# Rows of h_prime by a block transpose and a round trip through memory, fused masks in all batches, and the next batch's scores moved to the middle of a batch

## Chip, cores and metric

The kernel runs on one core of a Trainium2 chip. The time is the device time of one launch in microseconds (us); lower is better. The engines are PE (matmuls), DVE (vector), ACT (activations), POOL (GpSimd) and SP (here only a queue that issues DMAs).

## What is computed

Two graph layers over 16 batches of 1024 nodes with 128 features. `adj` is a symmetric 0/1 matrix per batch. Cut to what matters:

```
# layer 0, per batch
h = x @ Ww.T + Wb
e = (h @ A) @ h.T;  e = e + e.T
scores = where(adj > 0, e, 0)
attention = softmax(scores, axis=1) * adj
h_prime = relu(attention @ h)
ic, fc, oc = sigmoid(h_prime @ w_u + x @ w_x)        # three gates, one number per node each
x1 = layernorm(x + oc * tanh(ic * h_prime + fc * x))
# layer 1, per batch, 4 heads
h = x1 @ conv_w[hd] + conv_b[hd]
scores = h @ attn_w[hd] @ h.T
out += relu(tanh(adj * scores) @ h)
x2 = layernorm(x1 + relu(relu(out / 4) + x1))
```

Everything is float32.

## The kernel before

**Tiling.** The 1024 nodes of a batch are 8 blocks of 128 (NB = 8)[...]. A batch's adjacency is 8 tiles of 128x1024 (`adjp`, 16 buffers, so two batches). Only the pool `ps_sc` with four PSUM banks takes the results of the matmuls that are read at once; it is shared by scores, projections and small products. Two accumulators of two banks each (`acc0`, `acc1`) hold the products of layer 0 and layer 1.

**Order.** The order of instructions on each engine is the order in which the program is written; nothing is reordered afterwards. Waits between engines follow from the data and from the reuse of buffers.

**The main loop (lines 619 to 640).** For each batch b there are 32 steps, one for each head and row block. `layer1_step` multiplies one block of scores of layer 1 (PE, L510), weighs it by the adjacency (DVE, L511), takes the tanh (ACT, L512) and queues its product (PE, L516), which is issued two steps later (DELAY = 2). At the end of a head `add_head` (L528) adds the accumulator into the sum. Between the steps stand pieces of layer 0 of the following batch. They are functions with short names, and a table says which run after which step: BETWEEN (L609) for the batch b+1, AHEAD (L615) for the batch b+2, TURN (L616) for the step that turns x1, and ENDING (L617) for the four pieces of the last batch's end (turn of the sum, residual, statistics, normalisation and output).

**Pieces of layer 0** (function `layer0`; j is a row block):

- `L` loads xT and all eight adjacency tiles on SP's queue, `X` loads x.
- `Q0 Q1` project qT (PE, ACT). `H0 H1 H2` project h's rows (PE L272, DVE L273); three columns of the product are the gates' part from x.
- `Sj` makes a block row of scores from its diagonal on (PE L288, ACT L291). They are symmetric, so `Tj` (`turn_score`) brings the rest of block row j in transposed: a DVE transpose of 32x32 blocks (L313), a write to memory (L317) and four reads that set the blocks in place (L320), all on SP. Batch 0 uses PE for it.
- `Aj` (`mask`) masks the scores and takes their maximum. With an edge mask in hand (batch 0, made by `find_edges` on POOL, L328) this is one fused DVE operation (L338) with a read of its accumulator and a negation (L342); otherwise it is two DVE operations (L345, L346). Then ACT takes the exponential (L348).
- `Bj` (`weigh`) multiplies by the adjacency (DVE L353), scales h (L355, ACT L357) and issues the product for block j-1 (PE L365). `R` issues the last one and takes the relu into `hpT`, which has features on the partitions.
- `P`, `p` (`rows_hp`, L377): eight matmuls of `hpT` with `ident_g` (L384), an identity with the three gate columns beside it. They give h_prime with nodes on the partitions and h_prime's part of the gates in the same result; ACT copies them out (L385).
- `G` (`gates`): the sum of the gate parts, the sigmoids (ACT L392, DVE L393, L394) and, on POOL, fc * x (L398).
- `I0`, `O0`, `V0`, `N0`: the inner and outer steps (DVE L408, ACT L412, DVE L419) and the layernorm (statistics L184 to L188, a power on POOL L189, L192).

`turn_x1` and `layer1_end` use the helper `turn` (L221): a DVE transpose (L225), a write to memory (L227), four reads (L230), one directly after the other on SP's queue. SP takes its DMAs in order, and one that waits holds those behind it. Where buffers are few (`R`, `u`, `x`, `hp` one each, `turn` two), a piece waits for the last use of the tile.

Of the kernel before, what the change touches and what calls it, by code (L numbers as in the profile page):

```python
# [11 lines left out]
F32 = mybir.dt.float32  # L12
BF16 = mybir.dt.bfloat16
AF = mybir.ActivationFunctionType
# [4 lines left out]
P = 128  # L19
# [4 lines left out]
def two_layer_adjacency_kernel(  # L24
# [44 lines left out]
    a_in = consts.tile([P, P], F32, name="a_in")  # L69
    nc.sync.dma_start(a_in, A)  # L70
    ww_in = consts.tile([P, P], F32, name="ww_in")
# [19 lines left out]

    def load_late_weights():
        nc.sync.dma_start(cw_in[0:1], conv_b.rearrange("(o h) d -> o h d", o=1))
        nc.sync.dma_start(cw_in[1:P], conv_w[:, 0 : D - 1, :].rearrange("h f d -> f h d"))
        nc.sync.dma_start(cw_last, conv_w[:, D - 1 : D, :].rearrange("h f d -> f h d"))
        nc.sync.dma_start(aw, attn_w.rearrange("h i j -> i h j"))

# [6 lines left out]
    but_first = consts.tile([1, P], F32, name="but_first")  # L104
# [10 lines left out]
    a_sym = consts.tile([P, P], F32, name="a_sym")  # L115
    s_ww = consts.tile([P, P], F32, name="s_ww")
# [3 lines left out]
    b_wide = consts.tile([P, P], F32, name="b_wide")  # L120
# [98 lines left out]
    Q = 32  # L219

    def turn(dst, src, name):  # L221


        t = sb.tile([P, N], F32, tag="turn", name=f"turn_{name}", bufs=2)
        nc.vector.transpose(t.rearrange("p (k d) -> p k d", d=P), src)  # L225
        d = dram.tile([P, N], F32, tag="turn", name=f"dram_{name}")
        nc.sync.dma_start(d, t)  # L227
        dv = d.rearrange("(a i) (k c j) -> c i k a j", i=Q, c=P // Q, j=Q)
        for c in range(P // Q):
            nc.sync.dma_start(  # L230
                dst[ts(c, Q)].rearrange("i (k a j) -> i k a j", a=P // Q, j=Q), dv[c]
            )

    adj_t, x_t, x1_t = {}, {}, {}


    def layer0(b):
# [7 lines left out]
        def load():  # L245
            t["xT"] = sb.tile([P, N], F32, tag="xT", name=f"xT_{b}")
            nc.sync.dma_start(t["xT"], xT[b])
            adj_t[b] = []
            for j in range(NB):
                a = adjp.tile([P, N], F32, tag="adj", name=f"adj_{b}_{j}")  # L250
                nc.sync.dma_start(a, adjT[b, ts(j, P), :])
                adj_t[b].append(a)
# [44 lines left out]
        def turn_score(j):  # L297


            R, L, w = t["R"], NB - 1 - j, (NB - 1 - j) * P  # L300
            if b == 0:
                for l0 in range(0, L, 4):
                    ls = range(j + 1 + l0, min(j + 5 + l0, NB))
                    ps = small(f"turn0_{j}_{l0}")
                    for i, l in enumerate(ls):
                        nc.tensor.transpose(ps[:, ts(i, P)], R[:, l, j, :], ident)
                    nc.scalar.copy(
                        R[:, j, ls[0] : ls[-1] + 1, :],
                        ps[:, : len(ls) * P].rearrange("p (l d) -> p l d", d=P),
                    )  # L310
                return
            sq = sb.tile([P, N], F32, tag="turn", name=f"turn0_{b}_{j}", bufs=2)
            nc.vector.transpose(  # L313
                sq[:, :w].rearrange("p (l d) -> p l d", d=P), R[:, j + 1 :, j, :]
            )
            d = dram.tile([P, w], F32, tag=f"turn0_{j}", name=f"dram0_{b}_{j}")
            nc.sync.dma_start(d, sq[:, :w])  # L317
            dv = d.rearrange("(a i) (l c j) -> c i l a j", i=Q, c=P // Q, j=Q)
            for c in range(P // Q):
                nc.sync.dma_start(  # L320
                    R[ts(c, Q), j, j + 1 :, :].rearrange("i l (a j) -> i l a j", j=Q),
                    dv[c],
                )

        def find_edges(j):

            m = sb.tile([P, N], BF16, tag="h1", name=f"edge_{b}_{j}", bufs=NB + 1)
            nc.gpsimd.tensor_scalar(m, adj_t[b][j], 0.0, None, ALU.is_gt)  # L328
            t["edge", j] = m.rearrange("p (k d) -> p k d", d=P)

        def mask(j):
            s = t["R"][:, :, j, :]
            nmax = sb.tile([P, 1], F32, tag="nmax", name=f"nmax_{b}_{j}", bufs=4)
            if ("edge", j) in t:
                top = -3e38
                for q, ks in enumerate((ts(0, BH), ts(1, BH)) if j == 0 else [slice(NB)]):
                    highest = sb.tile([P, 1], F32, tag="highest", name=f"highest_{b}_{j}_{q}", bufs=4)
                    nc.vector.tensor_tensor_reduce(  # L338
                        s[:, ks], s[:, ks], t["edge", j][:, ks], 1.0, top, ALU.mult, ALU.max, highest
                    )  # L340
                    top = highest
                nc.vector.tensor_scalar_mul(nmax, highest, -1.0)  # L342
            else:
                adj = adj_t[b][j].rearrange("p (k d) -> p k d", d=P)
                nc.vector.scalar_tensor_tensor(s, adj, 0.0, s, op0=ALU.is_gt, op1=ALU.mult)  # L345
                nc.vector.tensor_reduce(nmax, s, AX.XY, ALU.max, negate=True)  # L346
            t["z", j] = sb.tile([P, 1], F32, tag="z", name=f"z_{b}_{j}", bufs=4)
            nc.scalar.activation(s, s, AF.Exp, bias=nmax, accum_out=t["z", j])  # L348

        def weigh(j):  # L350

            s = t["R"][:, :, j, :]
            nc.vector.tensor_mul(s, s, adj_t[b][j].rearrange("p (k d) -> p k d", d=P))  # L353
            rz = sb.tile([P, 1], F32, tag="rz", name=f"rz_{b}_{j}", bufs=4)
            nc.vector.reciprocal(rz, t["z", j])  # L355
            t["hz", j] = sb.tile([P, D], F32, tag="hz", name=f"hz_{b}_{j}", bufs=4)
            nc.scalar.mul(t["hz", j], t["h"][:, j, :D], rz)  # L357
            if j:
                back(j - 1)
# [27 lines left out]
        def gates():  # L387

            gate = t["gate"]
            gflat = gate.rearrange("p k g -> p (k g)")  # L390
            nc.vector.tensor_add(gate, t["hp"][:, :, D : D + 3], gate)
            nc.scalar.activation(gflat, gflat, AF.Exp, scale=-1.0)  # L392
            nc.vector.tensor_scalar_add(gflat, gflat, 1.0)  # L393
            nc.vector.reciprocal(gflat, gflat)  # L394
            t["u"] = sb.tile([P, NB, D], F32, tag="u", name=f"u0_{b}", bufs=1)
            t["x1"] = sb.tile([P, NB, D + 1], F32, tag="x1", name=f"x1_{b}")
            for ks in PARTS:
                nc.gpsimd.tensor_mul(  # L398
                    t["u"][:, ks], t["x"][:, ks],
                    gate[:, ks, 1:2].to_broadcast([P, ks.stop - ks.start, D]),  # L400
                )
            nc.gpsimd.memset(t["x1"][:, :, 0:1], 1.0)

# [21 lines left out]
        def finish(p):  # L425
# [7 lines left out]
            "L": load, "X": load_x, "R": relu,  # L433
            "P": lambda: rows_hp(GROUPS[:-1]), "p": lambda: rows_hp(GROUPS[-1:]),
            "G": gates,
        }
        for i, ks in enumerate(GROUPS):
            pieces[f"H{i}"] = partial(project_h, [ks])
# [7 lines left out]
        for j in range(NB):  # L446
            for name, piece in (("S", score), ("A", mask), ("B", weigh)):
                pieces[f"{name}{j}"] = partial(piece, j)
            if b == 0:
                pieces[f"E{j}"] = partial(find_edges, j)  # L450
# [10 lines left out]
    x1T_t, h1_t, u_t = {}, {}, {}  # L461

    def turn_x1(b):
        if b:
            x1T_t[b] = sb.tile([P, N], F32, tag="x1T", name=f"x1T_{b}")
            turn(x1T_t[b], x1_t[b][:, :, 0:D], f"x1_{b}")
            return
# [25 lines left out]
    def layer1_step(b, hd, m):  # L493
        x1T, h1, uT = x1T_t[b], h1_t[b, m], u_t[b, hd]
        adj = adj_t[b][m]
# [50 lines left out]
    def layer1_end(b):  # L546
        x1 = x1_t[b][:, :, 1 : D + 1]
        y = sb.tile([P, NB, D], F32, tag="u", name=f"y_{b}", bufs=1)
        turn(y.rearrange("p k d -> p (k d)"), sum_t[b].rearrange("p (k d) -> p k d", d=P), f"sum_{b}")
# [8 lines left out]
    def last_end(b, k0, k1):  # L558
# [19 lines left out]
    run(first, "L X")  # L578
    load_late_weights()
    run(second, "L")  # L580
# [8 lines left out]
    run(first, "P p G")  # L589
# [14 lines left out]
    run(second, "T0 T1 T2")  # L604
    rows(0, range(NB))

    BETWEEN = [  # L609
        "H0 H1 H2", "S0", "T0 S1", "T1 S2", "T2 A0", "S3 B0", "T3 A1", "S4 B1",  # L610
        "T4 A2", "S5 B2", "T5 A3", "S6 B3", "T6 A4", "S7 B4", "A5", "B5",
        "A6", "B6", "A7", "B7", "X R", "P", "p G", "I0",
        "O0", "V0", "N0", "", "", "", "", "",
    ]
    AHEAD = {28: "L", 31: "Q0 Q1"}  # L615
    TURN = 27  # L616
    ENDING = (DELAY, DELAY + 3, DELAY + 5, DELAY + 7)  # L617
    end, nxt = None, second
    for b in range(B):
        after = layer0(b + 2) if b + 2 < B else {}  # L620
        for step in range(H * NB):
            hd, m = divmod(step, NB)
            layer1_step(b, hd, m)
            if b and step == 0:
                rows(b, range(NB // 2, NB))
            if end is not None and step in ENDING:
                next(end, None)
            run(nxt, BETWEEN[step])
# [64 lines left out]
```

## Time and profile before

Three runs took 2447.58, 2448.38 and 2449.35 us, a median of 2448.38. The profiled run took 2446.58, and its span is 2444.8 us at a granted PE clock of 0.999.

| group (line) | count | us busy | mean ns of one |
|---|---|---|---|
| PE scores of layer 1 (L510) | 2048 | 962.0 | 592 |
| PE product of layer 1 (L516) | 2016 | 947.3 | 592 |
| PE product of layer 0 (L365) | 512 | 241.1 | 593 |
| PE rows of h_prime (L384) | 256 | 33.8 | 275 |
| DVE scores by adjacency (L511) | 1008 | 671.5 | 685 |
| DVE mask (L345) | 120 | 143.3 | 1195 |
| DVE maximum (L346) | 120 | 146.4 | 1220 |
| DVE fused mask, batch 0, 1024 wide (L338) | 7 | 8.5 | 1210 |
| DVE weights by adjacency (L353) | 128 | 158.7 | 1240 |
| POOL edges, batch 0 (L328) | 8 | 23.4 | 2950 |
| POOL fc * x, 1024 wide (L398) | 15 | 28.5 | 1900 |
| ACT copy of h_prime's rows, 393 wide (L385) | 32 | 15.6 | 488 |

A float32 matmul appears as two records. The time of one record is its latency; records that follow each other overlap, so that the mean of one is longer than the time it adds, and what it adds is the distance between two starts. In a list of waits the columns are the waiting instruction, what it waited for, the sum in us, how often, and the longest.

| DMA | queue | count | KB each | us to landing |
|---|---|---|---|---|
| adjacency tile | SP | 128 | 512 | 7.7 |
| xT | SP | 16 | 512 | 4.5 |
| x1's write, reads | SP | 15, 60 | 512, 128 | 2.6, 3.1 |
| output | POOL | 15 | 512 | 3.5 |

### The profile page before, as it was taken

The numbers are of one execution on the slowest core, as the hardware profiler recorded it, in microseconds if no ns is written. First come the engines' busy times: TensorE is split into PE (matmuls) and PEld (weight loads), VectorE is DVE, ScalarE is ACT, GpSimd is POOL, SyncE is SP. The second block draws the span as 40 slices with busy tenths as digits, with TensorE's granted clock in tenths as the row PEclk, the third lists the DMA queues.
The fourth block names the chain that finished last, engine by engine and source line by source line (L and its number), as shares of the span: only waits on it lengthen the run. The fifth ranks groups of instructions, "written<-read, shape, count | busy, mean of one in ns | idle before, by whom it ended". The sixth has DMA issues, their size and how long they took to land.

```text
span 2444.8 us, 19911 instructions
## 1 busy us (share of the span) xinstructions
PE 2427.2 (99%) x6175; PEld 1121.6 (46%) x6175; DVE 1585.3 (65%) x3026; ACT 1083.9 (44%) x1522; POOL 136.5 (6%) x102
## 2 busy tenths in 40 slices
PE   8999999999999999999999999999999999999998
PEld 4444444444444444444444444444444444444444
DVE  6665847657586565866658666585765857658454
ACT  6444444344444444434444444444444444444432
POOL 4000000000000000000000000000000000000000
PEclk9999999999999999999999999999999999999999
DMA  4204124051230512304133140332404223042000
GB/s 174 60 10 145 45 95 95 1 151 39 95 95 9 148 34 101 89 21 142 27 108 81 52 124 15 119 70 72 106 12 128 62 95 84 11 135 55 17 26 9
DMA packets 409057, 180.77 MB, mean 74 GB/s; under 512 B 352630, under 2 KB 377078, under 8 KB 408951
## 3 DMA queue, kind: packets, MB, share of 16 engines
q1 hardware_dynamic: 405927, 171.63, 25.2%
q0 software_dynamic: 2160, 7.87, 0.8%
q8 instruction: 49, 0.80, 0.1%
q14 instruction: 57, 0.47, 0.1%
q10 hardware_dynamic: 864, 0.00, 0.0%
HBM read 127.80 MB, written 51.64 MB: 73 GB/s over the span
## 4 chain that ended last, share of the span: by engine, by line
PE 94%; DVE 2%; DMA 2%; SPq 1%; issue 0%; POOL 0%; ACT 0%; POOLq 0%; DVEq 0%
PE sc L510 34%; PE acc L516 34%; PE acc L365 9%; PE sc L288 5%; PE pT_u L201 4%; PE pR L481 4%; PE pT_q L201 1%; PE pt L384 1%; PE pR_h L272 1%; DMA xT<-in_xT_dram 1%; SPq L230 1%; DMA dram_x<-turn_x 0%; DVE st L184 0%; DVE x L192 0%; POOL rs L189 0%
## 5 line engine op out<-in xcount | busy, mean ns | idle before, releaser
L511 DVE TENSOR_TENSOR s<-sc,adj 128x512 f32<-128x512 f32 x1008 | 671.5, 685 | 623.0 <-PE sc L510 611.0
L510 PE MATMUL sc<-uT,x1T 128*128 128x512 f32 x2048 | 962.0, 592 | 0.0
L516 PE MATMUL acc<-s,h 128*128 128x512 f32 x2016 | 947.3, 592 | 0.0
L512 ACT ACTIVATE s<-s 128x1024 f32<-128x1024 f32 x504 | 533.0, 1057 | 806.9 <-DVE s L511 800.5
L516 PEld LDWEIGHTS acc<-s,h 128*128 128x128 f32 x2016 | 381.7, 190 | 483.5 <-issue 474.4
L510 PEld LDWEIGHTS sc<-uT,x1T 128*128 128x128 f32 x2048 | 385.7, 190 | 468.8 <-issue 421.7
L365 PE MATMUL acc<-R,hz 128*128 128x512 f32 x512 | 241.1, 593 | 1.5 <-ACT hz L357 1.4
L348 ACT ACTIVATE R<-R,nmax 128x1024 f32<-128x1024 f32 x128 | 147.0, 1149 | 201.9 <-DVE nmax L346 182.2
L353 DVE TENSOR_TENSOR R<-R,adj 128x1024 f32<-128x1024 f32 x128 | 158.7, 1240 | 5.7 <-issue 0.3
L346 DVE TENSOR_REDUCE nmax<-R 128x1 f32<-128x1024 f32 x120 | 146.4, 1220 | 4.1
L288 PE MATMUL sc<-xT,qT 128*128 128x512 f32 (+3 forms) x384 | 146.5, 491 | 0.5 <-ACT R L291 0.5
L365 PEld LDWEIGHTS acc<-R,hz 128*128 128x128 f32 x512 | 95.6, 190 | 108.0 <-issue 85.1
L345 DVE SCALAR_TENSOR_TENSOR R<-adj,R 128x1024 f32<-128x1024 f32 x120 | 143.3, 1195 | 0.0
L189 POOL TENSOR_TENSOR rs<-rs,mhalf 128x8 f32<-128x8 f32 (+2 forms) x35 | 65.8, 1881 | 1207.0 <-DVE rs L188 948.3
L291 ACT ACTIVATE R<-sc,h 128x512 f32<-128x512 f32 (+1 forms) x192 | 109.4, 579 | 39.2 <-PE sc L288 37.7
L201 PE MATMUL pT_u<-x1T,ms 128*128 128x512 f32 x256 | 120.4, 592 | 0.0
L481 PE MATMUL pR<-cw,x1T 128*128 128x512 f32 x256 | 114.9, 592 | 0.0
L357 ACT ACTIVATE hz<-h,rz 128x128 f32<-128x128 f32 x128 | 51.3, 400 | 128.7 <-DVE rz L355 128.4
L288 PEld LDWEIGHTS sc<-xT,qT 128*128 128x128 f32 x384 | 70.1, 192 | 70.4 <-issue 58.0
L484 ACT COPY h<-pR 128x512 f32<-128x512 f32 x128 | 75.0, 586 | 41.7 <-PE pR L481 41.7
L398 POOL TENSOR_TENSOR u<-x,gate 128x1024 f32<-128x1024 f32 (+1 forms) x17 | 30.6, 1799 | 969.4 <-DVE gate L394 969.4
L534 DVE SCALAR_TENSOR_TENSOR sum<-acc,sum 128x512 f32<-128x512 f32 x95 | 61.2, 686 | 33.8 <-PE acc L516 32.9
(109 smaller groups left out, 1035.2 us busy)
## 6 DMA issues: line engine op xcount, KB each, us to landing
adj<-in_adjT_dram SPq DMA_DIRECT2D x128, 512.0 KB, 7.7
xT<-in_xT_dram SPq DMA_DIRECT2D x16, 512.0 KB, 4.5
x<-in_x_dram SPq DMA_DIRECT2D x16, 512.0 KB, 4.2
dram_x<-turn_x SPq DMA_DIRECT2D x15, 512.0 KB, 2.6
x1T<-dram_x SPq DMA_DIRECT2D x60, 128.0 KB, 3.1
dram_sum<-turn_sum SPq DMA_DIRECT2D x15, 512.0 KB, 2.6
y<-dram_sum SPq DMA_DIRECT2D x60, 128.0 KB, 3.1
out_dram<-y POOLq DMA_DIRECT2D x15, 512.0 KB, 3.5
```

The source lines that it names most:

```text
L201: nc.tensor.matmul(ps, w, src[:, ts(q, 512)], start=True, stop=True)
L288: nc.tensor.matmul(ps[:, : at - lo], t["qT"][:, ts(j, P)], t["xT"][:, lo:at], start=True, stop=True)
L345: nc.vector.scalar_tensor_tensor(s, adj, 0.0, s, op0=ALU.is_gt, op1=ALU.mult)
L346: nc.vector.tensor_reduce(nmax, s, AX.XY, ALU.max, negate=True)
L348: nc.scalar.activation(s, s, AF.Exp, bias=nmax, accum_out=t["z", j])
L353: nc.vector.tensor_mul(s, s, adj_t[b][j].rearrange("p (k d) -> p k d", d=P))
L365: nc.tensor.matmul(t["acc"][:, ts(q, 512)], t["hz", j], t["R"][:, ts(q, BH), j, :], start=(j == 0), stop=(j == NB - 1),)
L481: nc.tensor.matmul(ps, x1T_t[b][:, ts(k, P)], cw.rearrange("p h d -> p (h d)"), start=True, stop=True)
L510: nc.tensor.matmul(ps, x1T[:, ts(m, P)], uT[:, ts(q, 512)], start=True, stop=True)
L511: nc.vector.tensor_mul(s[:, ts(q, 512)], ps, adj[:, ts(q, 512)])
L512: nc.scalar.activation(s, s, AF.Tanh)
L516: nc.tensor.matmul(acc[:, ts(q, 512)], h1[:, ts(hd, D)], s[:, ts(q, 512)], start=(m == 0), stop=(m == NB - 1),)
```

## The change

1. **h_prime's rows.** In batches 1 to 15 `hpT` is turned as x1 is: DVE transpose, write, four reads (`turn_hp`, piece P). h_prime's part of the gates then comes from three weighted sums over the features: POOL multiplies by a gate's weights (`weigh_hp`), which are loaded once as rows on all partitions (`wu_b`), and DVE sums (`sum_hp`). The gates are finished in pieces Y, F, i and o. Batch 0 keeps the matmuls.
2. **Masks.** All batches use the fused operation; from batch 1 on the mask is uint8 with two buffers and is made per block (`E0` to `E7`) on POOL.
3. **Hops.** `hop` issues the write to memory and keeps the reads, which `land` issues a step later.
4. **Loads.** xT (W) and each adjacency tile (L0 to L7) are pieces of their own, and from batch 2 on the adjacency comes by POOL's queue.
5. **Plan.** The scores S and turns T of batch b+2 run in steps 15 to 22 of batch b (before: steps 1 to 13 of batch b+1); masks and weights run from step 29 on into steps 0 to 10. The first loop has a plan of its own (FIRST). ENDING is 2, 6, 11, 13 instead of 2, 5, 7, 9.
6. **Buffers.** Some weight tiles of the preparation move into shared buffers.

```diff
+    wu_b = consts.tile([P, 3, D], F32, name="wu_b")
...
+        for g, w in enumerate((wi_u, wf_u, wo_u)):
+            nc.sync.dma_start(wu_b[:, g, :], w.partition_broadcast(P))
...
+    def hop(dst, t, name):
+        d = dram.tile(list(t.shape), F32, tag=f"hop_{t.shape[1]}", name=f"dram_{name}")
+        nc.sync.dma_start(d, t)
+        dv = d.rearrange("(a i) (k c j) -> c i k a j", i=Q, c=P // Q, j=Q)
+        def read():
+            for c in range(P // Q):
+                nc.sync.dma_start(
+                    dst[ts(c, Q)].rearrange("i k (a j) -> i k a j", a=P // Q), dv[c]
+                )
+        hops.append(read)
+    def land():
+        while hops:
+            hops.popleft()()
...
+        def load_adj(j):
+            a = adj_t[b, j] = adjp.tile([P, N], F32, tag="adj", name=f"adj_{b}_{j}")
+            (nc.sync if b < 2 else nc.gpsimd).dma_start(a, adjT[b, ts(j, P), :])
...
         def find_edges(j):
-            m = sb.tile([P, N], BF16, tag="h1", name=f"edge_{b}_{j}", bufs=NB + 1)
-            nc.gpsimd.tensor_scalar(m, adj_t[b][j], 0.0, None, ALU.is_gt)
+            if b == 0:
+                m = sb.tile([P, N], BF16, tag="h1", name=f"edge_{b}_{j}", bufs=NB + 1)
+            else:
+                m = sb.tile([P, N], U8, tag="edge", name=f"edge_{b}_{j}")
+            nc.gpsimd.tensor_scalar(m, adj_t[b, j], 0.0, None, ALU.is_gt)
...
-                nc.vector.scalar_tensor_tensor(s, adj, 0.0, s, op0=ALU.is_gt, op1=ALU.mult)
-                nc.vector.tensor_reduce(nmax, s, AX.XY, ALU.max, negate=True)
+                nc.vector.tensor_tensor_reduce(
+                    s[:, ks], s[:, ks], t["edge", j][:, ks], 1.0, nmax, ALU.mult, ALU.max, top
+                )
...
+        def turn_hp():
+            t["hp"] = sb.tile([P, NB, D], F32, tag="hp", name=f"hp_{b}", bufs=1)
+            hpT = t["hpT"].rearrange("p (k d) -> p k d", d=P)
+            turn(t["hp"], hpT, f"hp_{b}")
+        def weigh_hp(g):
+            if b not in x1T_t:
+                x1T_t[b] = sb.tile([P, N], F32, tag="x1T", name=f"x1T_{b}")
+            t["hw"] = x1T_t[b].rearrange("p (k d) -> p k d", d=P)
+            nc.gpsimd.tensor_mul(
+                t["hw"], t["hp"], wu_b[:, g : g + 1, :].to_broadcast([P, NB, D])
+            )
+        def sum_hp(g):
+            hw = sb.tile([P, NB, 1], F32, tag="hw", name=f"hws_{b}_{g}")
+            nc.vector.tensor_reduce(hw, t["hw"], AX.X, ALU.add)
+            gate = t["gate"][:, :, g : g + 1]
+            nc.vector.tensor_add(gate, hw, gate)
...
+        def gate_f():
+            sum_hp(1)
+            sigmoid(t["gate"][:, :, 1:2])
+            forget()
+            weigh_hp(0)
+        def gate_i():
+            sum_hp(0)
+            weigh_hp(2)
+        def gates_io():
+            sum_hp(2)
+            sigmoid(t["gate"][:, :, 0:3:2])
...
-    run(second, "T0 T1 T2")
+    run(second, "T0 T1")
+    land()
+    run(second, "T2 E0")
     rows(0, range(NB))
+    land()
...
-    BETWEEN = [
-        "H0 H1 H2", "S0", "T0 S1", "T1 S2", "T2 A0", "S3 B0", "T3 A1", "S4 B1",
-        "T4 A2", "S5 B2", "T5 A3", "S6 B3", "T6 A4", "S7 B4", "A5", "B5",
-        "A6", "B6", "A7", "B7", "X R", "P", "p G", "I0",
-        "O0", "V0", "N0", "", "", "", "", "",
-    ]
-    AHEAD = {28: "L", 31: "Q0 Q1"}
-    TURN = 27
-    ENDING = (DELAY, DELAY + 3, DELAY + 5, DELAY + 7)
+    BETWEEN = {
+        0: "L7 E5 B1 A3", 1: "B2", 2: "E6 A4", 3: "E7 B3 A5", 4: "A6", 5: "B4", 7: "B5 A7",
+        8: "B6", 10: "B7", 11: "X R", 12: "P", 14: "Y", 16: "F", 18: "i", 20: "o", 21: "I0",
+        22: "O0", 23: "V0", 24: "N0",
+    }
+    AHEAD = {
+        9: "W", 12: "Q0 Q1", 14: "H0 H1 H2", 15: "S0", 16: "T0 S1", 17: "T1 S2", 18: "T2 S3",
+        19: "T3 S4", 20: "T4 S5", 21: "T5 S6", 22: "T6 S7", 25: "L0", 26: "L1", 27: "L2 E0",
+        28: "L3 E1", 29: "L4 A0 E2", 30: "L5 A1 E3", 31: "L6 B0 A2 E4",
+    }
+    FIRST = {
+        0: "E1 A0 T3 S4", 1: "E2 B0 A1 T4 S5", 2: "E3 A2 T5 S6", 3: "E4 B1 A3 T6 S7",
+        4: "E5 B2 A4", 5: "E6 B3 A5", 6: "E7 B4 A6", 7: "B5 A7",
+    }
+    TURN = 25
+    ENDING = (DELAY, 6, 11, 13)
...
         for step in range(H * NB):
             hd, m = divmod(step, NB)
             layer1_step(b, hd, m)
+            land()
```

## The prediction

> **What bounds the kernel now.** I read the page first: busy time by engine, then the chain that ended last.
>
> ```profile
> span 2444.8 us, 19911 instructions
> PE 2427.2 (99%) x6175; PEld 1121.6 (46%) x6175; DVE 1585.3 (65%) x3026; ACT 1083.9 (44%) x1522; POOL 136.5 (6%) x102
> PE 94%; DVE 2%; DMA 2%; SPq 1%; issue 0%; POOL 0%; ACT 0%; POOLq 0%; DVEq 0%
> ```
>
> PE is busy for all but 17.6 us of 2444.8, and 94% of the last chain is PE. A busy PE need not be at its peak, so I next looked at the timeline of PE around the rows of h_prime, at about 1066 us.
>
> ```profile
> 1064.32 1.88 PE L516 MATMUL acc<-s,h 128*128 128x512 f32 x4
> 1066.03 1.50 PE L384 MATMUL pt<-ident_g,hpT 128*128 128x131 f32 x12
> 1067.37 1.88 PE L510 MATMUL sc<-uT,x1T 128*128 128x512 f32 x4
> 1069.09 1.88 PE L516 MATMUL acc<-s,h 128*128 128x512 f32 x4
> 1070.81 0.61 PE L384 MATMUL pt<-ident_g,hpT 128*128 128x131 f32 x4
> 1071.25 1.88 PE L510 MATMUL sc<-uT,x1T 128*128 128x512 f32 x4
> ```
>
> The columns are start and length. Lengths overlap, so the price of an operation is the distance between starts: four 512-wide records take 1.717 us (0.429 each), twelve L384 records 1.34 us and four 0.44 us (0.1115 each). The same 1.717 us stands between all 512-wide groups of this batch. Nothing is lost between instructions. Third, PE's waits; these are the longest:
>
> ```profile
> PE pw L122 <- DMA a_in<-in_L_gnn_A_dram: 3.2, 1, 3.2
> PE pt L565 <- DVE sum L534: 1.6, 1, 1.6
> PE pT_q L201 <- DMA xT<-in_xT_dram: 1.6, 5, 0.7
> PE acc L365 <- ACT hz L357: 1.4, 4, 0.5
> ```
>
> L122 is the kernel's start and L565 its end. In the loop almost only the xT wait is left. So the time is PE's work, one record after another. Work on other engines counts only if it makes PE wait. Last, how much PE forgives: DVE's timeline where I0, O0, V0 and N0 run now.
>
> ```profile
> 1077.12 1.28 DVE L511 TENSOR_TENSOR s<-sc,adj 128x512 f32<-128x512 f32 x2
> 1078.32 2.18 DVE L419 SCALAR_TENSOR_TENSOR u<-u,gate,x 128x128 f32<-128x128 f32 x8
> 1080.42 1.28 DVE L511 TENSOR_TENSOR s<-sc,adj 128x512 f32<-128x512 f32 x2
> 1081.75 1.29 DVE L534 SCALAR_TENSOR_TENSOR sum<-acc,sum 128x512 f32<-128x512 f32 x2
> 1082.96 1.64 DVE L184 BATCH_NORM_STATS2 st<-u 128x6 f32<-128x128 f32 x8
> 1084.51 0.63 DVE L186 BATCH_NORM_AGGREGATE mv<-st 128x2 f32<-128x6 f32 x8
> ```
>
> DVE works here without a gap. The step of 1080 to 1085 has 5.0 us of DVE work against 3.43 us of PE work (scores and product of one step, 2 x 1.717), and PE still does not wait. Lateness of about 1.9 us is therefore free.
>
> [...] L353 (two SBUF inputs) has a median of 1.218 us and a longest of 1.854, where POOL's L328 ran beside it, and L189 on POOL takes 1.67 or 2.48 us; L511, with one input in PSUM, never passes 0.693. [...] The trace's only such DMA, the output, holds POOL 0.97 us and lands after 3.5.
>
> **The change, part by part.** Made against the profile's span of 2444.8; its run took 2446.6, the three others 2447.6 to 2449.4 with a median of 2448.4, so the difference is laid on 2448.4.
>
> *h_prime by a turn.* In 15 of 16 batches the 16 L384 records go: 240 x 0.1115 = 26.8 us, all on the path. ACT loses its copies L385 (2 x 0.488 + 0.378 = 1.35 us a batch). Added per batch: one DVE transpose (1.23 us, row L225), one write and four reads on SP, three POOL products (1.90 us each by L398, 5.7), three DVE sums over 128x1024 (1.22 each by L346) with three small adds (0.18), and two sigmoids in place of one. About 5.9 us of DVE. Is it hidden? Step 12 transposes. A hop of the same size, x1, takes from 1090.45 (transpose) to 1094.37 (write landed), then 2.74 us of issuing and 3.1 to land: 9.8 us. From late in step 12 it lands near the start of step 14 plus 2 us; POOL's product adds 1.9, and DVE asks in step 16. Steps 14 and 15 hold 3.43 us each plus H0 to H2 (1.8) and S0 (1.72), so about 8 us are to spare. The next product (u and the product, 3.8 us on POOL) is asked for two steps later, with about 3 us to spare. Cost: nothing, hidden by PE's own queue.
>
> *Fused masks.* In 120 masks L345 and L346 (1.195 + 1.220) become one fused operation (1.210, row L338, as batch 0 runs it), an accumulator read (0.08) and a negation (0.153): DVE loses 0.97 us each, 117 us in all, none on PE's path. The uint8 mask is not in the trace. Low end for an edge on POOL: 2.85 us, the bf16 median; high end twice that. I take 2.9: the same elements are read. Per batch POOL gets 8 x 2.9 + 5.7 + 8 issues of about 1 = 37 us, of about 152.
>
> *Adjacency loads on POOL's queue.* L0 to L7 go one per step from 25, L0 waiting for step 24's products. Behind each waiting load on POOL stand the edges, and for those the masks wait on DVE. An adj load of before lands in 7.7 us with eight at once. E0 (step 27) then starts near 27 + 2.6 us; E0, L3, E1 take 2 x 2.9 + 1 = 6.8; the second mask is wanted three steps (10.3 us) after step 27, at 30 + 2.3. Spare: over 3 us. With two mask buffers E(j) also waits for mask j-2; the masks stand at 29, 30, 31, 0, 2, 3, 4, 7, so by the same count every edge has 2 us or more to spare. SP loses eight loads of 0.54 us and no longer waits for DVE's products.
>
> *Scores, turns and xT moved.* Same matmuls, transposes and SP writes and reads (five DMAs per turn), now from step 12, with 'land' issuing the reads a step later, so SP holds a blocked read less often. xT is asked for at step 9 and used at 12 (4.5 us to land against over 10): the xT wait goes. L201's pT_q records average 620 ns against 592 elsewhere, over 64 records 1.8 us; with the wait listed I take 2 us off. The crowded steps are now 21 to 25: DVE 5 x 1.28 + 2.19 + 2.18 + 2.44 + 2.14 + 1.29 + 1.23 + 0.73 (T5, T6) = 18.6 us; PE 5 x 3.43 + 0.65 = 17.8. Lateness 0.8 us; the same pieces now, in 23 to 27, give 17.9 against 17.2, or 0.7. No wait follows. The preparation gets three small broadcasts on SP: nothing or 1 us.
>
> *Sum.* -26.8 - 2 + 0 = -28.8; 2448.4 - 28.8 = 2419.6, said as **2420 us** (-1.2%).
>
> **The rivals.** *A, PE just does less* (0.77): 2420, own range 2415 to 2425. Low end: all loop waits go and the preparation gains 2; high end: the new chains cost PE 0.3 us a batch.
>
> *B, part is given back* (0.12): POOL's operations hold DVE's two-input ones up to 0.64 us each, as on L353; with 11 of them a batch that is 7 us of DVE, and where it meets step 16 or steps 2 to 4, PE waits about 1 us a batch: +15, 2435. For it: the 1.854 us. Against it: those steps have 4.2 us of DVE work to 4.9 to 5.2 of PE.
>
> *C, slower, POOL is the bound of the masks* (0.07): place, E0, L3, E1 ahead of the mask in step 30. If an edge with its uint8 store takes E us, the chain is late by 2E + 1 - 10.3. PE forgives about one step, 3.4 us, as its scores have four PSUM buffers and a step fills two. PE waits from E = 6.4, and the gain is gone from E = 7.3 (1.8 us a batch). At 8 us: 2 x 8 + 1 - 13.7 = 3.3 us, 15 times, 2420 + 50 = 2470. A load that lands 7 us late through POOL's queue does the same. For it: both are unseen. Against it: it needs 2.5 times the bf16 edge.
>
> *D, no difference* (0.04): losses of B's kind at 1.8 us a batch, 2448. That the change doesn't do what it says is no likely case, as the matmuls leave the text of the program.
>
> **How the numbers follow.** Time: A's. Range 2415 to 2432: A whole, and B up to 0.8 us a batch, some 0.8 of the chance. A measurement of this kernel can tell about 0.2% (5 us) from nothing: faster is A and B, 0.89; same is D, 0.04; slower is C, 0.07.
>
> **What would show it.** PE's busy time near 2400 with 5935 records; the rows' matmuls x16 instead of x256; the xT wait gone; PE's waits in the loop still under 0.5 us each; DVE about 30 us less busy; POOL near 680 us; edges near 2.9 us. It is wrong if PE waits for DVE or ACT in most batches, if edges take over 6 us, or if loads from POOL's queue land after 12 us or more.

## The result and the profile after

The changed kernel takes 2421.55 us (four runs, 2421.19 to 2423.47) against 2448.86 us of the kernel before, measured beside it. The ratio is 0.989, 95% interval 0.9873 to 0.9908. The prediction was 2420 us with a range of 2415 to 2432.

The page of the changed kernel, busy time and chain:

```profile
span 2419.2 us, 20097 instructions
PE 2400.6 (99%) x5935; PEld 1094.6 (45%) x5935; DVE 1552.1 (64%) x3266; ACT 1070.7 (44%) x1492; POOL 625.5 (26%) x379
PE 97%; DMA 1%; SPq 1%; DVE 1%; ACT 0%; issue 0%; POOL 0%; POOLq 0%; ACTq 0%; DVEq 0%
```

PE has 240 records fewer and is busy 26.6 us less; the span of the profiled run is 25.6 us shorter (the profiled run before was a quick one, so the medians differ by 27.3). PE is idle for 17.6 us in all before and 18.6 after. POOL's busy time has grown from 136.5 to 625.5 us without any of it showing in the span.

PE's waits after, the longest first (sum, number, longest):

```profile
PE pw L128 <- DMA a_in<-in_L_gnn_A_dram: 3.2, 1, 3.2
PE pt L614 <- DVE sum L583: 1.6, 1, 1.6
PE pt L521 <- DVE x L198: 1.5, 2, 1.0
PE acc L374 <- ACT hz L366: 1.3, 4, 0.5
PE pT_q L207 <- DMA xT<-in_xT_dram: 1.1, 1, 1.1
```

L128 is the kernel's start and L614 its end. The wait for xT has left the loop: the one that remains (1.1 us) is in the preparation, as are L521 and L374. By this list one wait is left in the loop, 0.8 us at L559, once, in the first batch. The timeline of PE shows one thing that the list leaves out, at the end of a batch (step 31):

```profile
952.85 1.88 PE L565 MATMUL acc<-s,h 128*128 128x512 f32 x4
954.56 1.88 PE L207 MATMUL pT_u<-x1T,ms 128*128 128x512 f32 x4
956.28 3.76 PE L530 MATMUL pR<-cw,x1T 128*128 128x512 f32 x8
959.88 1.88 PE L559 MATMUL sc<-uT,x1T 128*128 128x512 f32 x4
```

The eight records of L530 are the rows of layer 1 for the next batch. Eight records of 512 columns should be followed after 3.43 us (8 x 0.429); here it is 3.60. In the kernel before it was 3.43:

```profile
955.20 3.60 PE L481 MATMUL pR<-cw,x1T 128*128 128x512 f32 x8
958.63 1.88 PE L510 MATMUL sc<-uT,x1T 128*128 128x512 f32 x4
```

So 0.17 us is lost in each of 14 batches, 2.4 us in all. ACT's timeline at that moment:

```profile
956.29 1.15 ACT L357 ACTIVATE R<-R,nmax 128x1024 f32<-128x1024 f32 x1 [0.92 <-DVE nmax L355]
957.35 0.19 ACT L357 ACTIVATION_READ_ACCUMULATOR R<-R,nmax 128x1 f32 x1
957.44 1.05 ACT L209 COPY uT<-pT_u 128x512 f32<-128x512 f32 x2
958.38 2.28 ACT L533 COPY h<-pR 128x512 f32<-128x512 f32 x4
```

The copies of uT (L209) empty two of the four PSUM buffers that the rows' matmuls need. They are written in the program after the exponential of piece A2 (L357) and wait behind it. A loss of 0.17 us looks like nothing; the experiments show that at this place the new plan has no slack at all.

POOL's groups after (count, busy us, mean ns of one, idle time before it):

```profile
L343 POOL TENSOR_SCALAR edge<-adj 128x1024 uint8<-128x1024 f32 x120 | 332.7, 2772 | 320.6 <-DVE top_None L350 316.6 <-DMA R<-dram_turn 1.6
L406 POOL TENSOR_TENSOR x1T<-hp,wu_b 128x1024 f32<-128x1024 f32 x45 | 106.4, 2363 | 107.7 <-DVE hws L412 63.7 <-DVE s L560 39.5 <-DMA hp<-dram_hp 4.0
L271 POOL DMA_DIRECT2D adj<-in_adjT_dram x112 | 65.6, 586 | 92.5 <-DVE s L560 92.5
```

A uint8 edge takes 2.77 us (the bf16 one of batch 0 takes 2.93 in the same trace), a product 2.36 (1.90 was assumed), a load 0.59 to issue and 4.0 to land.

### The profile page after: what moved, and what is told of

The parts are those of the page before. It is cut to its first block, busy times and chain, and to the rows that moved or that the text cites. A ratio compares the mean times of both kernels' runs of the same rounds, so it can differ in the third digit from the quotient of the medians.

```text
span 2419.2 us, 20097 instructions
## 1 busy us (share of the span) xinstructions
PE 2400.6 (99%) x5935; PEld 1094.6 (45%) x5935; DVE 1552.1 (64%) x3266; ACT 1070.7 (44%) x1492; POOL 625.5 (26%) x379
## 4 chain that ended last, share of the span: by engine, by line
PE 97%; DMA 1%; SPq 1%; DVE 1%; ACT 0%; issue 0%; POOL 0%; POOLq 0%; ACTq 0%; DVEq 0%
PE sc L559 36%; PE acc L565 36%; PE acc L374 9%; PE pR L530 5%; PE pT_u L207 5%; PE sc L307 4%; PE pT_q L207 1%; PE pR_h L291 1%; SPq L99 1%; DMA xT<-in_xT_dram 0%; DMA adj<-in_adjT_dram 0%; PE acc_end L588 0%; SPq L97 0%; DMA R<-dram_turn 0%; DMA dram_turn<-turn 0%
## 5 line engine op out<-in xcount | busy, mean ns | idle before, releaser
L560 DVE TENSOR_TENSOR s<-sc,adj 128x512 f32<-128x512 f32 x1008 | 685.1, 688 | 716.4 <-PE sc L559 693.6
L559 PE MATMUL sc<-uT,x1T 128*128 128x512 f32 x2048 | 962.9, 593 | 0.9 <-ACT R L310 0.8
L559 PEld LDWEIGHTS sc<-uT,x1T 128*128 128x128 f32 x2048 | 387.4, 190 | 470.3 <-issue 403.4
L343 POOL TENSOR_SCALAR edge<-adj 128x1024 uint8<-128x1024 f32 (+1 forms) x128 | 355.9, 2782 | 327.7 <-DVE top_None L350 316.6
L195 POOL TENSOR_TENSOR rs<-rs,mhalf 128x8 f32<-128x8 f32 (+2 forms) x35 | 54.6, 1560 | 947.4 <-DVE rs L194 947.4
L374 PE MATMUL acc<-R,hz 128*128 128x512 f32 x512 | 241.0, 594 | 1.3 <-ACT hz L366 1.3
L357 ACT ACTIVATE R<-R,nmax 128x1024 f32<-128x1024 f32 x128 | 147.0, 1148 | 73.4 <-DVE nmax L355 69.0
L362 DVE TENSOR_TENSOR R<-R,adj 128x1024 f32<-128x1024 f32 x128 | 158.2, 1236 | 1.1 <-ACT R L357 0.7
L350 DVE CUSTOM_DVE_ANT_0 R<-R,edge 128x1024 f32<-128x1024 f32 (+1 forms) x128 | 154.2, 1205 | 3.3 <-PE turn L325 3.2
L374 PEld LDWEIGHTS acc<-R,hz 128*128 128x128 f32 x512 | 97.0, 190 | 123.9 <-issue 115.8
L406 POOL TENSOR_TENSOR x1T<-hp,wu_b 128x1024 f32<-128x1024 f32 x45 | 106.4, 2363 | 107.7 <-DVE hws L412 63.7
L530 PE MATMUL pR<-cw,x1T 128*128 128x512 f32 x256 | 117.3, 598 | 0.0
L271 POOL DMA_DIRECT2D adj<-in_adjT_dram x112 | 65.6, 586 | 92.5 <-DVE s L560 92.5
```

Source lines behind the costliest of these rows:

```text
L343: nc.gpsimd.tensor_scalar(m, adj_t[b, j], 0.0, None, ALU.is_gt)
L350: nc.vector.tensor_tensor_reduce(s[:, ks], s[:, ks], t["edge", j][:, ks], 1.0, nmax, ALU.mult, ALU.max, top)
L362: nc.vector.tensor_mul(s, s, adj_t[b, j].rearrange("p (k d) -> p k d", d=P))
L374: nc.tensor.matmul(t["acc"][:, ts(q, 512)], t["hz", j], t["R"][:, ts(q, BH), j, :], start=(j == 0), stop=(j == NB - 1),)
L530: nc.tensor.matmul(ps, x1T_t[b][:, ts(k, P)], cw.rearrange("p h d -> p (h d)"), start=True, stop=True)
L559: nc.tensor.matmul(ps, x1T[:, ts(m, P)], uT[:, ts(q, 512)], start=True, stop=True)
```

## The experiments

Times stand against 2421.55 us of the changed kernel. The runs were made in several sets, and the kernel before, run beside each, had medians from 2446.4 to 2449.2 us, so a difference of 2 or 3 us from the changed kernel is not told from none. The expectations call "theory one" what the prediction built on: PE's records alone set the time, and DVE's lateness of up to two or three microseconds is free wherever it is. "Theory two" was formed from the trace after: what is free depends on the place, and at step 31 it is nothing.

### h_prime's rows back on PE

```diff
-        if b == 0:
-            pieces.update(P=lambda: rows_hp(GROUPS), G=gates)
-        else:
-            pieces.update(P=turn_hp, Y=partial(weigh_hp, 1), F=gate_f, i=gate_i, o=gates_io)
+        pieces.update(P=lambda: rows_hp(GROUPS), G=gates)
...
-    16: "F"
+    16: "G"
```

> The changed kernel with one part undone: h_prime's rows and gate parts of all batches by matmuls again (the products Y, i, o and the turn of h_prime are gone, the gates follow in step 16). Theory one, only PE's own records set the time: 240 records of 0.1117 us come back, +26.8 us, so 2421.6 + 26.8 = 2448 us, the time of the kernel before. Rival, the new plan or the fused masks brought a share of the gain: then this kernel stays clearly under the kernel before, say 2440 us or less.

Measured: 2449.0 us, ratio to the kernel before 1.0003 (0.9996 to 1.001), 27.4 us over the changed kernel. The other parts of the change together (fused masks, hops in two halves, loads on POOL, moved scores) give nothing by themselves that this comparison can tell (its interval is about -1 to +2.5 us). The gain is the 240 records.

### The turn of h_prime in the old plan

```diff
-    BETWEEN = {0: "L7 E5 B1 A3", ... 12: "P", 14: "Y", 16: "F", 18: "i", 20: "o", 21: "I0", ... 24: "N0"}
-    AHEAD = {9: "W", 12: "Q0 Q1", ... 31: "L6 B0 A2 E4"}
-    TURN = 25
+    BETWEEN = {0: "L7 H0 H1 H2", 1: "S0 E0", ... 20: "X R", 21: "P", 23: "Y", 24: "F", 25: "i",
+               26: "o", 27: "I0", 28: "O0", 29: "V0", 30: "N0"}
+    AHEAD = {25: "L0", 26: "L1", 27: "L2", 28: "L3 W", 29: "L4", 30: "L5", 31: "L6 Q0 Q1"}
+    TURN = 30
```

> The changed kernel with the order of before: scores of the next batch from step 1 on, the turn of h_prime at 21, Y at 23, F, i, o at 24 to 26, I0 to N0 at 27 to 30, x1's turn at 30. Theory: the hop of h_prime fits only if all before it moved; here x1T, which takes a hop of about 10 us, is asked for by PE 3.4 us after step 31 begins. PE waits 7 to 10 us in 15 batches: 2421.6 + 105 to 150 = 2525 to 2570 us. Rival, the moved scores don't matter (the saved matmuls alone bring the gain): 2422 us, within 5.

The first loop's own plan (FIRST) is left out as well. Measured: 2669.6 us (one run), 248 us over the changed kernel. PE's waits in it:

```profile
PE pT_u L207 <- DMA x1T<-dram_x: 191.2, 15, 13.8
PE acc L565 <- DVE sum L583: 16.7, 15, 3.4
```

and the timeline of PE at one of them:

```profile
1044.78 3.56 PE L207 MATMUL pT_u<-x1T,ms 128*128 128x512 f32 x4 [12.70 <-DMA x1T<-dram_x]
1048.17 3.60 PE L530 MATMUL pR<-cw,x1T 128*128 128x512 f32 x8
```

So the moved scores are no gain in themselves (the run before), but in the one placement tried here the turn without them costs far more than it saves: from the relu (R) to the inner step (I0) the matmuls needed three steps and the turn has ten in the new plan; squeezed into seven, as here, it still pushes x1's turn to step 30, and x1's hop ends long after PE has asked for it. The estimate of 7 to 10 us per batch was short of the 12.7 us seen here. There is a second price, too: the four records behind the wait take 3.39 us from start to start and not 1.72. PE comes out of this wait at a lower rate (the granted clock of this run is 0.959, that of the changed kernel 0.999; more on this at the run with DVE work in step 24). PE is idle 208.7 us more than in the changed kernel and busy 39.7 us more for the same 5935 records; the two make up the 248.

### Two-operation masks, and A2 issued later

Three kernels: the old mask (two DVE operations, no edges on POOL) in the new plan; the piece A2 with its edge E4 issued behind `head_uT` and `rows`, not ahead of them; and both.

```diff
 # the old mask, batches 1 to 15
+                nc.vector.scalar_tensor_tensor(s, adj, 0.0, s, op0=ALU.is_gt, op1=ALU.mult)
+                nc.vector.tensor_reduce(nmax, s, AX.XY, ALU.max, negate=True)
 # A2 later
-    31: "L6 B0 A2 E4"
+    31: "L6 B0"
...
                     head_uT(b + 1, 0)
                     rows(b + 1, range(NB // 2))
+                    run(after, "A2 E4")
```

> The changed kernel with the two-operation mask of before in batches 1 to 15 and no edges on POOL; all else as changed. Theory one, as in the prediction, 0.97 us more of DVE per mask is free because PE forgives lateness of about 2 to 3.4 us: 2421.6 us, within 2. Theory two, lateness is not free where ACT has the exponential of A2 ahead of uT's copies (step 31): nmax of A2 comes 1.0 us later, PE waits 1.0 us more in each of 14 batches: 2436 us.

> The changed kernel with pieces A2 and E4 of step 31 issued after the next batch's head_uT and rows, not ahead of them. In the changed kernel's trace PE loses 0.17 us a batch before the rows' third matmul, where ACT has the exponential of A2 in front of uT's copies. Theory two, that order is the cause: the 14 losses go, -2.3 us, 2419.3 us. If the cause is another (PSUM buffers held by DVE), the losses stay and the time is 2421.6 us.

> Two-operation masks and no edges as in the run before, and A2 issued after head_uT and rows. Theory two: the late exponential stands behind the copies and delays nothing, 2420 us, within 2. If two-operation masks cost time in another place (steps 0 to 7, DVE as the bound), this kernel is as slow as the one with two-operation masks alone, about 2436 us. Theory one gives 2421 for both.

Measured: two-operation masks 2442.55 us, +21.0; A2 later 2420.39 us, -1.2; both 2421.53 us, no difference. PE's longest wait with the old masks:

```profile
PE pR L539 <- ACT uT L209: 17.6, 14, 1.3
```

and ACT in that kernel at one of the 14:

```profile
966.99 1.15 ACT L355 ACTIVATE R<-R,nmax 128x1024 f32<-128x1024 f32 x1 [1.98 <-DVE nmax L353]
968.04 0.19 ACT L355 ACTIVATION_READ_ACCUMULATOR R<-R,nmax 128x1 f32 x1
968.14 1.05 ACT L209 COPY uT<-pT_u 128x512 f32<-128x512 f32 x2
```

ACT stands idle for 1.98 us in front of A2's exponential, with the copies of uT behind it. The old masks make the maximum late, and as A0, A1 and A2 follow in three steps, A2's exponential is 1.36 us later against PE than in the changed kernel, and not the 1.0 us of one mask. The later A2 takes the price away. That edit changes nothing but ACT's order: `head_uT` and `rows` hold no DVE and no POOL instruction, so A2's mask and E4 keep their places there. So it is the order on ACT and no other load that costs. Theory one falls: DVE's longer masks are not free in this plan. Theory two's place is shown; its size was too small. Between the starts of PE's records, 19.0 of the 21.0 us are lost at these rows (1.36 a batch, not 1.0), and the other 2.1 in two waits of the first loop.

A2 later alone (ratio to before 0.9889, 0.9875 to 0.9904) is not parted from the changed kernel by its interval. The profile does show that the 0.17 us a batch are gone (2.4 us in all):

```profile
956.51 3.60 PE L530 MATMUL pR<-cw,x1T 128*128 128x512 f32 x8
959.95 1.88 PE L559 MATMUL sc<-uT,x1T 128*128 128x512 f32 x4
```

Its preparation, which the edit doesn't touch, took 1.1 us longer in that execution (the first product of the loop's uT starts at 62.97 us and not at 61.90), and its span is 2418.1 us against 2419.2.

### Slower edges

```diff
-            nc.gpsimd.tensor_scalar(m, adj_t[b, j], 0.0, None, ALU.is_gt)
+            for _ in range(2 if b else 1):      # 3 in the last of the runs
+                nc.gpsimd.tensor_scalar(m, adj_t[b, j], 0.0, None, ALU.is_gt)
```

> The changed kernel with each uint8 edge mask made twice on POOL (same result), so an edge costs 5.54 us and not 2.77. Theory one, by the prediction's rival C: PE waits only from 6.4 us on, so nothing, 2421.6 us. Theory two: the third edge is made only after A0 and then ends 1.6 us after DVE asks for it in A2 (step 31), A2's exponential holds uT's copies on ACT, PE waits about 1.6 us in 14 batches: 2444 us.

> Edges of 5.54 us and A2 with E4 issued after head_uT and rows. Theory two: the late A2 is off PE's way, 2420 us, within 3. If slow edges cost by holding DVE (its products of the scores behind A2), the time stays near 2440. Theory one gives 2420 as well, but also for the run before.

> Each uint8 edge made three times, 8.3 us. Theory one, the formula of rival C: (2 x 8.3 + 1 - 13.7) = 3.9 us a batch, 2421.6 + 58 = 2480 us. Theory two, from the changed kernel's trace: A1 asks 5.6 us too early, A2 then 9.5 us and A6 some 4 us more, about 13 us a batch: 2610 us.

Measured: doubled 2477.21 us, +55.7 (ratio to before 1.0127, 1.011 to 1.0144); doubled with A2 later 2421.13 us, no difference; threefold 2649.27 us (one run), +228. In the doubled one PE waits at the same place:

```profile
PE pR L531 <- ACT uT L209: 36.3, 14, 2.6
```

DVE's timeline there:

```profile
973.92 1.22 DVE L363 TENSOR_TENSOR R<-R,adj 128x1024 f32<-128x1024 f32 x1
975.05 0.16 DVE L365 RECIPROCAL rz<-z 128x1 f32<-128x1 f32 x1
977.80 1.22 DVE L351 CUSTOM_DVE_ANT_0 R<-R,edge 128x1024 f32<-128x1024 f32 x1 [2.59 <-POOL edge L344]
```

and POOL's:

```profile
965.12 5.78 POOL L344 TENSOR_SCALAR edge<-adj 128x1024 uint8<-128x1024 f32 x2
970.85 0.60 POOL L271 DMA_DIRECT2D adj<-in_adjT_dram  x1
971.48 6.28 POOL L344 TENSOR_SCALAR edge<-adj 128x1024 uint8<-128x1024 f32 x2
```

POOL has no gap from E0 to E2, and A2's mask waits 2.59 us for its edge; one microsecond more than was worked out, as E0, E1 and E2 took 5.65, 5.78 and 6.28 us and not 5.54 each. PE's waits are not the whole price: PE is also busy 18.3 us more for the same records (the next experiment shows why). That and the microsecond in each of 14 batches are nearly all of what lies between theory two's 2444 and the 2477 measured. The same edges cost nothing when A2's exponential stands behind the copies. So it is neither POOL's load nor DVE's wait that costs, but what ACT has behind the late piece. The threefold run is 39 us over theory two. PE waits most for the copies of uT (121.8 us), but also for the scores' PSUM buffers; its 228 us are the sum of several such places and of the lower rate (granted clock 0.97), which I did not take apart.

### Extra DVE work in two places

Four reductions of x1 (1.21 us each; their results are not used) at the end of step 24, or of step 27.

```diff
+            if step == 24 and b + 1 < B:        # or 27
+                for _ in range(4):
+                    hw = sb.tile([P, NB, 1], F32, tag="hw", name=f"dose_{b}")
+                    nc.vector.tensor_reduce(hw, x1_t[b + 1][:, :, 1 : D + 1], AX.X, ALU.max)
```

> The changed kernel with four DVE reductions of x1 (1.21 us each, results unused) added at the end of step 24: 4.84 us of lateness. Theory one, PE forgives 3.4 us wherever it is: 4.84 + 0.8 - 3.4 = 2.2 us in 15 batches, 2455 us. Theory two, the head's sum in step 25 has only about 1.2 us, as layer 1's accumulator has one buffer and the next head's first product waits for it: 3.6 us in 15 batches, 2475 us.

> The same four DVE reductions at the end of step 27, away from a head's end. Theory one: DVE is up to date there, 4.84 - 3.4 = 1.4 us in 15 batches, 2443 us. Theory two: only the four PSUM buffers of the scores count, with DVE's idle time of the step about 5 us free, 2422 us, within 3.

Measured (one run each): 2515.57 us in step 24, +94; 2422.53 us in step 27, +1.0, within the spread of the changed kernel's own runs. The same 4.6 us of DVE work (that is what the four take together) are free in one place and cost 6.3 us in the other. PE's timeline in step 26 of the first:

```profile
966.13 1.88 PE L559 MATMUL sc<-uT,x1T 128*128 128x512 f32 x4
971.83 3.41 PE L565 MATMUL acc<-s,h 128*128 128x512 f32 x4 [3.82 <-DVE sum L583]
975.08 1.88 PE L559 MATMUL sc<-uT,x1T 128*128 128x512 f32 x4
```

The wait is for the head's sum: layer 1 has one accumulator, and the next head's first product writes it. That was theory two's place and size (3.6 us expected, 3.82 seen). The rest of the 94 us is in the line itself: the four records take 3.25 us from start to start. The table of stretches for the same kernel gives the clock (PEclk, the third number from the end, as a share of the full clock):

```profile
960.00:968.00 8.00, 8.00 (x19) 3.23 (x17) 7.34 (x22) 1.06 (x1) 2.25 (x2) 1.00 0.39 91
972.00:975.00 3.00, 3.00 (x4) 1.29 (x5) 2.01 (x3) 0.90 (x1) 0.67 (x2) 0.54 0.84 292
976.00:984.00 8.00, 8.00 (x20) 3.55 (x19) 3.60 (x6) 2.11 (x2) 5.63 (x4) 1.00 0.75 188
```

Behind this wait of 3.8 us PE ran for some three microseconds at 0.54 of its clock. Fifteen waits of 3.85 us on average are 57.7 us; the slow records behind them make up nearly all of the other 36 (PE is busy 35.7 us more for the same 5935 records). In the three microseconds behind these waits the clock was between 0.50 and 0.58 in fourteen batches and 0.71 in one. Behind the doubled edges PE's wait was 2.59 us in each of 14 batches, and in the three microseconds after it the clock was between 0.53 and 0.70 in ten of them and 1.00 in four. Two of these in the kernel with doubled edges:

```profile
981.00:984.00 3.00, 2.99 (x5) 1.38 (x6) 0.00 (x0) 2.10 (x5) 2.92 (x2) 0.68 0.00 0
1134.00:1137.00 3.00, 2.83 (x7) 1.40 (x8) 0.00 (x0) 2.65 (x6) 2.92 (x2) 1.00 0.03 12
```

So the clock fell behind some waits of 2.59 us and not behind others, and the length of the wait alone did not decide whether it fell. What else did is not shown.

### The adjacency loads back on SP's queue

```diff
-            (nc.sync if b < 2 else nc.gpsimd).dma_start(a, adjT[b, ts(j, P), :])
+            nc.sync.dma_start(a, adjT[b, ts(j, P), :])
```

> The changed kernel with the adjacency loads of batches 2 to 15 on SP's queue, at the same steps. Theory one and two: the loads wait for products that are done by then and stand between hops that have microseconds to spare; 2421.6 us, within 2. Rival, the queue matters (a load that waits on DVE holds SP's hop of x1 behind it): PE waits for x1T at step 31, from 1 us a batch, 2437 us or more.

> Adjacency loads on SP's queue and, in addition, A2 and E4 issued after head_uT and rows. With the loads on SP alone the profile shows them held behind x1's hop on that queue, the edges and A2 late by 0.9 us at step 31, and PE's wait for uT's copies 0.9 us a batch. Theory two, that this one place is the whole price of the queue: 2420.5 us, within 1.5. If the loads on SP cost elsewhere too (the hops held behind the loads, x1T late), the time stays near 2432 us.

Measured: 2432.14 us, +10.6 (ratio to before 0.9931, 0.9914 to 0.9947); with A2 later 2420.17 us, no difference. SP's queue in the first:

```profile
943.91 1.49 SPq L271 DMA_DIRECT2D adj<-in_adjT_dram  x1
946.96 3.50 SPq L237 DMA_DIRECT2D x1T<-dram_x  x4
950.51 11.26 SPq L271 DMA_DIRECT2D adj<-in_adjT_dram  x7
```

The rival was right that the queue matters, and wrong on the way: x1T is in time. The read of x1's hop waits for its write, is issued at 946.96, 1.56 us behind L0, and holds the loads L1 to L7 behind it until 950.51. The edges come late, A1 and A2 with them, and PE waits 0.88 us at the rows of this batch (8.1 us in 13 waits by the list), once more through ACT's order. In this batch A1's mask waited 0.76 us for its edge and then took 2.04 us itself in place of 1.21, while POOL was making edges (8.23 us of them from 955.16); so a part of the lateness (0.83 us) is what rival B had named. Both theories had set this run at no difference; theory two knew the place but I had not followed the queue to it.

## Why the prediction was right, point by point

- **The removed matmuls.** 240 records at 0.1115 us, -26.8: busy time fell by 26.6, and putting them back cost 27.4 us. This term is the result.
- **The wait for xT.** -2 was taken; it left the loop, and between the starts of PE's records 3.2 us went with it. Against it stand 2.4 us at the rows, which the prediction did not have, 1.2 us before L559 in the first loop (0.8 of it is one wait in the list, where the prediction had every wait of the loop under 0.5) and 0.6 us net in the preparation, where nothing or 1 us was allowed for. So the span fell by 25.6 us and not by 28.8, and the median by 27.3. That gains and losses of 2 to 3 us nearly cancelled was luck.
- **The hop of h_prime.** The prediction gave it about 8 us to spare. In the trace the transpose starts at 873.72, POOL's product ends at 886.43 and DVE's sum starts at 894.41: 8.0 us to spare. The second product ends at 900.92 and is asked for at 904.07: 3.1 us to spare, with 3 said.
- **Crowded steps 21 to 25.** Lateness of 0.8 us and no wait: PE runs through them without a gap. Right, but nearer to the edge than was thought: the step-24 run shows that the slack ahead of the head's sum is about 0.8 us (4.6 us of work, 3.82 us of waiting).
- **Other engines.** DVE 33 us less busy (30 said), POOL 625 us (680 said: loads are issued in 0.59 us and not 1, edges take 2.77 and not 2.9, while the products take more). Rival B's lengthened operations hardly came: in the loop no fused mask (L350) took over 1.23 us and no weighing (L362) over 1.22.
- **What was wrong: the step "Lateness of about 1.9 us is therefore free", and with it rival C's point.** I read the slack at one place of the old plan and used it for all of the new one. Even there it was misread: 5.0 us of work against 3.43 are 1.6 us, and with the lateness that DVE brought along it was 2.6 (PE starts that step's scores at 1081.55, DVE takes them at 1085.25, where 1.06 us is the distance when DVE is on time). C was to need an edge of 7.3 us to lose the gain; edges of 5.7 to 6.3 us made the kernel slower than before. The chain of C was placed at the mask of step 30; the one that decides is A2 in step 31, through ACT. For the same reason "none on PE's path" is too much for the fused masks: by themselves they bring nothing, yet in this plan they spare 21 us, and the loads on POOL's queue spare 10.6.

The forecast was right because its main term was right and because, at the measured durations, the tightest place was overrun by only 0.17 us a batch. That the masks and loads were such that A2 came no later was not reasoned out: in that the forecast was lucky, and its margin for the edges was smaller than it said.

## What to carry to other kernels

Here PE hardly ever waited, so removing its own records paid in full, and the rest of the change is judged by whether it lets that happen: parts that measure as nothing by themselves can still be conditions. Slack is not a number of an engine but of a place: for each step, ask what stands behind the late instruction on its own engine, and which buffer PE asks for next; here one exponential in front of two copies turned 1 to 3 us of lateness on DVE or POOL into waits of PE, and putting it behind them made the old masks, doubled edges or loads on another queue free again. The loss of 0.17 us per batch in the timeline was the first sign of it.

## What had not been expected of the hardware

A wait of PE can cost more than its length: behind 3.8 us of waiting the next four records took 3.25 us in place of 1.72 (granted clock 0.54), and behind 12.7 us they took 3.39. Behind the same 2.59 us they took from 1.82 to 3.43 in the 14 batches of one run. With waits of 1.3 us (two-operation masks) they took 1.82, at a granted clock of 1.00. A product of two tiles on POOL with one operand repeated over the blocks took 2.36 us where a similar one takes 1.91 in the same kernel; no run here says why.
